# First layer of a sparse graph-attention kernel: whole-array transposes and Gram products with PSUM banks shared by two readers, in place of row tiles with one reader for each pair of banks

## Chip, cores and metric

The kernel runs on one core of a Trainium2 chip. The metric is the device time of one execution in microseconds; a run's time is that of its slowest core, here the only one. Before the change three runs took 906.34, 911.70 and 915.76 us, median 911.7.

## The reference

A two-layer graph attention block with residual and layer norms: 8 batches, 2048 nodes, 64 features, 4 heads of width 64. Cut to what matters:

```python
def _gat_layer(h, mask, b):
    scores = einsum('...nd,...md->...nm', h, h)
    attn = softmax(where(mask, scores, NEG))
    return einsum('...nm,...md->...nd', attn, h) + b
mask = adj + eye(N) > 0
h = einsum('bnc,hdc->bhnd', x, Wh)                 # first layer, 4 heads
z = leaky_relu(concat_heads(_gat_layer(h, mask, bh)), 0.2)
h2 = einsum('bnk,dk->bnd', z, Wo)                  # second layer, one head
z2 = leaky_relu(_gat_layer(h2, mask, bo), 0.2)
out = layernorm(x + layernorm(z2) * gamma + beta)
```

The adjacency matrix is random and uneven: the first nodes have many neighbours (hubs), the others few.

## The kernel before

The fast path is `fast_kernel`. The first 56 nodes are hubs and are handled densely. The other 1992 are cut into 166 sets of 12 nodes; each set has a list of at most 128 nodes that any of its members is linked to, found on VectorE (DVE) by repeated top-8 searches over packed bit keys (`pick`). A set's rows of x, all 8 batches at once, are fetched by an indirect DMA on the GpSimd queue (POOL, `gather`), 128 rows of 520 floats.

Four stages follow each other: the hub stage (dense scores of the hubs against all nodes, making of keys, first searches), the loop of the first layer, its drain, and the second layer. The change is in the first two.

The loop of the first layer (lines 1038 to 1106) handles one group g of two sets per iteration, 83 groups, with a software pipeline: iteration i has in hand the scores of group i+1, the values of group i, the transposes of group i+3 and so on. The order of the work on each engine is the order in which the program writes it. In one iteration TensorE (PE) does, in this order:

- `scores` (line 836): 16 matmuls in two row tiles of 64x128 (128 keys stationary, 48 columns moving), from `xTg`, the transposed rows, and `y`, the nodes' own features times the Gram matrices of the heads. They write the pair of PSUM banks `S`; `weigh` on DVE reads it, `lift` on ScalarE (ACT) exponentiates.
- `project` (line 538): eight 64x64 matmuls of 96 columns into the pair `C`; `leaky` (line 525) on ACT reads it, `leak` on DVE applies the slope.
- `columns` (line 819): eight 64x64 matmuls of 96 columns, the Gram matrices on the own rows, into the pair `T`; `keep_columns` on ACT copies them to `y`. The own rows come from `own_rows` on POOL, every second iteration, in three copies, two of them from one half of the partitions to the other (line 811).
- `second_maps` (line 895), `values` (line 861: 16 matmuls in column tiles of 128x64, 65 columns) and `second_rows` (line 911) into the pair `O`; `keep_own`, `invert` and `keep_rows` on DVE read it.
- `turn` (line 514): the gathered rows of two sets are transposed in 16 half transposes (64x128 stationary, 64 columns moving) into `T`; the next iteration copies them to `xTg` on ACT (line 1045).
- `turn_values` (line 880): eight transposes of 48 rows into the free columns of `C`; `keep_values` on ACT reads them.

An fp32 matmul appears as two passes in the trace, each with its own weight load; a transpose is one pass. PSUM has eight banks of 512 floats per partition, and the four pairs `S`, `C`, `T`, `O` take them all, each pair existing once. Before the change each pair is read by one engine: `S` and `O` by DVE, `C` and `T` by ACT. Before the change, also, the two gathers of a group are held back by explicit dependencies: the first until the scores of the iteration are done, the second until half of its values are (lines 1055 and 1075). Twelve row buffers exist.

DVE also works off the searches, a few steps per iteration (`some`), SP issues the loads of adjacency pieces (`load_adj`), of own rows for the residual (`load_own`) and the stores of the second layer's table, and POOL adds beta (`add_beta`, line 949).

Of the kernel before, what the change touches and what calls it, by code (L numbers as in the profile page):

```python
# [359 lines left out]
def fast_kernel(ctx: ExitStack, tc: tile.TileContext, x, adj, Wh, bh, Wo, bo, gamma, beta, out, flag):  # L360
# [29 lines left out]
    rowp = stage.enter_context(tc.tile_pool(name="rowp", bufs=12))  # L390
# [118 lines left out]
    def turn(tp, rows, j=0):  # L509

        for q in range(Q):
            c0 = (j * Q + q) * 64
            for r in range(2):
                nc.tensor.transpose(tp[:, r, c0:c0 + 64], rows[half(r), q, 1:1 + P], ident[half(r), half(r)])  # L514

    def turn_whole(tp, rows):

        for q in range(Q):
            nc.tensor.transpose(tp[:, q * P:(q + 1) * P], rows[:, q, 1:1 + P], ident)  # L519
# [12 lines left out]
    def project(ot, cat, n):  # L532

        for hp in range(HP):
            for s in range(2):
                for j in range(2):
                    h = 2 * hp + j
                    at = nc.tensor.matmul(cat[half(j), s, hp * n:(hp + 1) * n], whT[half(s), h * D:(h + 1) * D],  # L538
                                          ot[half(s), h, :], start=True, stop=True)
        return at  # L540
# [47 lines left out]
    def turn_x(i):  # L588
        tp = two(f"px{i}")
        turn(tp, xrow[i])  # L590
        nc.scalar.copy(xT[:, :, i * P:(i + 1) * P].rearrange("c q (r n) -> c r q n", r=2),
                       tp[:, :, :Q * 64].rearrange("c r (q n) -> c r q n", q=Q))
# [141 lines left out]
    def pick(r):  # L734
# [7 lines left out]
        def top(src, dst, last):  # L742
            todo.append(lambda: nc.vector.max(out=dst, in_=src))
            if not last:
                todo.append(lambda: nc.vector.match_replace(out=src, in_to_replace=dst, in_values=src, imm_value=-1.0))

        for j in range(ns):
            for i in range(KEEP // 8):
                k = j * KEEP + i * 8
                top(kv[:, j, :], cand[:, k:k + 8], i == KEEP // 8 - 1)  # L750
# [7 lines left out]
        for i in range(P // 8):  # L758
            top(cand, best[:, i * 8:(i + 1) * 8], i == P // 8 - 1)
# [35 lines left out]
    def gather(table, s, layer, new, behind=None):  # L795
        t = rows[layer, s] = new(f"g{layer}_{s}")
        g = nc.gpsimd.indirect_dma_start(out=t.rearrange("n q c -> n (q c)"), out_offset=None, in_=table,  # L797
                                         in_offset=bass.IndirectOffsetOnAxis(ap=index[:, s:s + 1], axis=0))
        if behind is not None:
            tc.add_manual_dep(g.ins, behind.ins.name, mybir.DependencyInfo(mybir.DependencyClass.Sync, mybir.DependencyReason.DATA),  # L800
                              reason="the gather's turn")

    def own_rows(m):

        t = held["x", m] = work.tile([P, 2 * GM], F32, tag="xo", name=f"xo{m}", bufs=2)
        v = t.rearrange("c (b s q k) -> c b s q k", b=2, s=2, q=Q)
        src = xT[:, :, HUB:].rearrange("c q (k s) -> c s q k", s=NS)
        nc.gpsimd.tensor_copy(v[:, 0], src[:, 4 * m:4 * m + 2])
        b0 = min(4 * m + 2, NS - 2)
        for r in range(2):  # L810
            nc.gpsimd.tensor_copy(v[half(r), 1], src[half(1 - r), b0:b0 + 2])  # L811

    def columns(g, tp):

        t = held["x", g // 2]
        for k in range(2):
            for r in range(2):
                for p in range(2):
                    nc.tensor.matmul(tp[half(p), r, k * GM:(k + 1) * GM], gram[half(r), g % 2 * 2 + k, half(r)],  # L819
                                     t[half(r), (p ^ r) * GM:((p ^ r) + 1) * GM], start=True, stop=True)  # L820

    def keep_columns(g, tp):
        if g % 2 == 0:
            held["y", g // 2] = work.tile([P, 2 * GM, H], F32, tag="yg", name=f"y{g // 2}", bufs=2)
        h0 = g % 2 * 2
        nc.scalar.copy(held["y", g // 2].rearrange("p (b n) h -> p b n h", b=2)[:, :, :, h0:h0 + 2],  # L826
                       tp[:, :, :2 * GM].rearrange("p b (k n) -> p b n k", k=2))

    def scores(g, sp):
        xt = held.pop(("T", 1, g))  # L830
        y = held["y", g // 2].rearrange("p n h -> p (n h)")
        for j in range(2):
            for q in range(Q):
                for p in range(2):
                    c0 = ((g % 2) ^ p) * GM * H + (j * Q + q) * M
                    at = nc.tensor.matmul(sp[:, p, (q * 2 + j) * M:(q * 2 + j + 1) * M], xt[half(p), j, q, :],  # L836
                                          y[half(p), c0:c0 + M], start=True, stop=True)
        return at
# [12 lines left out]
    OW = D + 2  # L851

    def values(g, op):
        e = es[g % 2]
        rw = [rows.pop((1, 2 * g + j)) for j in range(2)]
        for q in range(Q):
            for j in range(2):
                for p in range(2):
                    c0 = (p * 8 + q * 2 + j) * M
                    o0 = q * OW + p  # L860
                    at = nc.tensor.matmul(op[half(p), j, o0:o0 + K1], e[:, c0:c0 + 64], rw[j][:, q, sums(p)], start=True, stop=True)  # L861
                    if (q, j, p) == (1, 1, 1):
                        midway = at
        return midway

    def invert(g, op):
        v = op[:, :, :Q * OW].rearrange("a j (q c) -> a j q c", q=Q)
        osb = held["o", g] = work.tile([P, 2, Q, D], F32, tag="osb", name=f"osb{g}")
        r = rall[:, g, :].rearrange("a (j q) -> a j q", j=2)
        for p in range(2):  # L870
            nc.vector.reciprocal(r[half(p)], v[half(p), :, :, p * K1])
        nc.vector.tensor_tensor(osb, v[:, :, :, 1:K1], r.unsqueeze(3).to_broadcast([P, 2, Q, D]), OP.mult)  # L872

    def turn_values(g, pt):

        osb = held.pop(("o", g)).rearrange("a j q c -> a (j q c)")
        for w in range(4):
            for p in range(2):
                mine = slice(p * 64, p * 64 + M)
                at = nc.tensor.transpose(pt[:, p, w * M:(w + 1) * M], osb[mine, w * P:(w + 1) * P], ident[mine, mine])  # L880
        return at

    def keep_values(g, pt):

        ot = held["ot", g] = work.tile([P, H, GM], F32, tag="ot", name=f"otb{g}")
        nc.scalar.copy(ot.rearrange("c h (p m) -> c p h m", p=2), pt.rearrange("c p (m h) -> c p h m", h=H))  # L886
# [14 lines left out]

    def store_own(g):

        t = held["own", g]
# [3 lines left out]
    def second_rows(g, pr):  # L908
        t = held.pop(("own", g))
        for r in range(2):  # L910
            nc.tensor.transpose(pr[:, r, :], t[half(r)], ident[half(r), half(r)])  # L911

    def keep_rows(g, pr):
        r = rowts[g % 4]
        nc.vector.tensor_tensor(r[:GM, 1:1 + P].rearrange("n (p d) -> n p d", p=2), pr, bob[:GM], OP.add)
# [63 lines left out]
    for i in range(NB):  # L979
# [16 lines left out]
        for t in range(2):  # L996
# [12 lines left out]
            some(6)  # L1009
# [4 lines left out]
    for g in range(3):  # L1014
# [23 lines left out]
    for i in range(-4, NG + 4):  # L1038
        if i >= 1 and slow and len(slow) % 3:
            slow.pop(0)()  # L1040
        sp = one(f"s{i + 1}", "S")
        scored = scores(i + 1, sp) if 0 <= i + 1 < NG else None
        if 0 <= i + 2 < NG:
            t = held["T", 1, i + 2] = work.tile([P, 2, Q, P], F32, tag="xTg", name=f"xTg{i + 2}", bufs=2)
            nc.scalar.copy(t.rearrange("c j q (r n) -> c r (j q) n", r=2),  # L1045
                           held.pop(("tp", i + 2)).rearrange("c r (m n) -> c r m n", n=64))
        cat = one(f"cat{i}", "C")
        if 0 <= i - 2 < NG:
            project(held.pop(("ot", i - 2)), cat, GM)
            held["z", i - 2] = leaky(cat, GM, f"z{i - 2}")  # L1050
        if 0 <= i + 1 < NG:
            weigh(i + 1, sp)
        coming = i + LOOK if i > -3 else NG
        if coming < NG:
            gather(table1, 2 * coming, 1, rows_tile, scored)
        if turns():
            some(1)
        if i >= 0:
            if slow and len(slow) % 3 == 0:
# [4 lines left out]
        tp = one(f"t{i + 3}", "T")  # L1064
        if 0 <= i + 4 < NG + NG % 2:
            columns(i + 4, tp)
            keep_columns(i + 4, tp)
        if 0 <= i + 1 < NG:
            lift(i + 1)
        op = one(f"o{i}", "O")  # L1070
        if 0 <= i - 3 < NG:
            second_maps(i - 3, op[:, 0, 264:264 + GM])
        midway = values(i, op) if 0 <= i < NG else None
        if coming < NG:
            gather(table1, 2 * coming + 1, 1, rows_tile, midway)
        if 0 <= i - 4 < NG:
            second_rows(i - 4, op[:GM, :, 360:424])
        if 0 <= i - 2 < NG:
            leak(held["z", i - 2])
        if 0 <= i - 3 < NG:  # L1080
            keep_own(i - 3, op[:, 0, 264:264 + GM])
            store_own(i - 3)
        if i + 6 < NG and i % 2 == 0 and i >= -2:
            own_rows((i + 6) // 2)
        if i >= 10 and (i - 10) // 6 * 2 + (i - 10) % 6 // 2 <= NV and (i - 10) % 6 < 4:
            (add_beta if i % 2 else load_own)((i - 10) // 6 * 2 + (i - 10) % 6 // 2)
        if 0 <= i < NG:
            invert(i, op)
        if 0 <= i - 4 < NG:
            keep_rows(i - 4, op[:GM, :, 360:424])  # L1090
        for _ in range(6 if i < 0 else 3 if i < 16 else 2):
# [365 lines left out]
```

## Time and profile before

| | |
|---|---|
| time of the profiled execution | 906.34 us (the median of three runs is 911.7) |
| span of the profile | 904.5 us, 40409 instructions |
| busy: PE / weight loads / DVE / ACT / POOL | 769.5 / 698.0 / 615.1 / 513.4 / 487.5 us |
| mean granted TensorE clock | 0.924 |
| scores, line 836 | 2656 passes, 169.6 us busy |
| values, line 861 | 2656 passes, 96.5 us busy |
| half transposes, line 514 | 1328, 57.9 us busy |
| columns, line 819 | 1328 passes, 54.8 us busy |
| transposes of values, line 880 | 664, 33.8 us busy |
| whole transposes of the second layer, line 519 | 664, 82.0 us busy |
| gathers, line 797 | 332, 994 ns each on POOL |

The profile gives, for each engine, busy time; idle time is put down to what ended it. PE's matmuls are pipelined, so the busy time of a matmul overlaps that of its neighbours; distances between start times tell what one costs in a row of its like. The chain of waits follows the program back from its last instruction and lists, for each stretch of time, the work that everything after it waited for. The granted clock is TensorE's, as a share of full speed.

### The profile page before, as it was taken

What the parts mean: (1) busy time and instruction counts of PE and PEld (TensorE: products, weight loads), DVE (VectorE), ACT (ScalarE), POOL (GpSimd) and SP (SyncE); (2) the same over time, 40 slices, a digit from 0 to 9 for tenths busy, and PEclk for the clock granted to TensorE, in tenths of its full rate; (3) what the DMA queues carried; (4) which work ended last, traced back from release to release, by engine and by line L of the source; (5) the groups of instructions that cost most, each with busy time, mean ns of one, the idle gap of its engine ahead of it and who ended that gap; (6) DMA issues with size and microseconds to landing.
All of it is one profiled execution on the core that took longest, in us unless ns stands there. A gap on an engine that the chain in (4) does not pass through costs nothing.

```text
span 904.5 us, 40409 instructions
## 1 busy us (share of the span) xinstructions
PE 769.5 (85%) x17676; PEld 698.0 (77%) x17676; DVE 615.1 (68%) x1369; ACT 513.4 (57%) x878; POOL 487.5 (54%) x696
## 2 busy tenths in 40 slices
PE   2896776889889999999999999994799999998720
PEld 2675565778779999999999999993699989997720
DVE  3347867447677787767655556655338899999993
ACT  2332243345446666666666666662477887887721
POOL 5643140436555566655556665631777777777300
PEclk9998797669999999999999999997799999999965
DMA  8786350335444555555445455431888888888521
GB/s 176 227 239 201 107 149 4 98 101 146 112 129 130 143 142 148 149 156 143 136 127 153 140 152 153 138 83 43 255 273 248 268 263 270 270 252 249 170 49 30
DMA packets 81787, 145.11 MB, mean 160 GB/s; under 512 B 30146, under 2 KB 46466, under 8 KB 81602
## 3 DMA queue, kind: packets, MB, share of 16 engines
q0 software_dynamic: 26720, 88.55, 34.3%
q1 hardware_dynamic: 37842, 49.65, 18.0%
q10 hardware_dynamic: 17040, 4.25, 2.5%
q8 instruction: 140, 2.29, 1.0%
q14 instruction: 45, 0.37, 0.1%
HBM read 123.91 MB, written 18.48 MB: 157 GB/s over the span
## 4 chain that ended last, share of the span: by engine, by line
PE 61%; DVE 14%; DMA 11%; issue 4%; ACT 4%; POOL 2%; SPq 2%; DVEq 0%; POOLq 0%; ACTq 0%
PE s L836 15%; PE o L861 8%; DMA g<-table,index 5%; PE t L514 4%; PE t L819 4%; PE o L895 4%; PE cat L538 4%; DMA raw<-in_adj_dram 4%; PE t L519 4%; PE s L1156 3%; PE o L1188 3%; PE sh L1300 2%; PE cat L880 2%; PE e L1167 2%; PE o L911 2%
## 5 line engine op out<-in xcount | busy, mean ns | idle before, releaser
L797 POOL DMA_INDIRECT g<-table,index x332 | 330.1, 994 | 136.6 <-issue 54.3
L836 PE MATMUL s<-y,xTg 64*128 64x48 f32 x2656 | 169.6, 280 | 0.8 <-DVE rowt L660 0.8
L836 PEld LDWEIGHTS s<-y,xTg 64*128 64x128 f32 x2656 | 164.0, 197 | 1.7 <-DVE rowt L660 1.2
L842 DVE TENSOR_TENSOR e<-s,mask 128x768 f32<-128x768 f32 x83 | 79.3, 956 | 50.7 <-PE s L836 47.5
L525 ACT ACTIVATE z<-cat,bhp 128x192 f32<-128x192 f32 x166 | 60.9, 418 | 84.6 <-PE cat L538 79.3
L861 PE MATMUL o<-g,e 128*64 128x65 f32 x2656 | 96.5, 228 | 0.0
L519 PE MATMUL t<-ident,g 128*128 128x128 f32 x664 | 82.0, 277 | 12.8 <-DMA g<-table,index 12.8
L861 PEld LDWEIGHTS o<-g,e 128*64 128x64 f32 x2656 | 91.3, 144 | 0.6 <-issue 0.4
L811 POOL COPY xo<-xT 64x96 f32<-64x96 f32 x84 | 30.1, 359 | 113.5 <-DMA g<-table,index 101.5
L1343 ACT COPY xTg<-t 128x1024 f32<-128x1024 f32 x83 | 80.1, 1016 | 17.1 <-PE t L519 16.5
L1045 ACT COPY xTg<-t 128x1024 f32<-128x1024 f32 x83 | 84.4, 1017 | 2.9 <-PE t L514 2.9
L519 PEld LDWEIGHTS t<-ident,g 128*128 128x128 f32 x664 | 75.0, 143 | 14.2 <-issue 9.1
L849 ACT ACTIVATE e<-e,shifts 128x768 f32<-128x768 f32 x83 | 78.1, 941 | 0.7 <-DVE e L842 0.7
L886 ACT COPY otb<-cat 128x384 f32<-128x384 f32 x83 | 39.8, 479 | 66.5 <-PE cat L880 66.5
L604 ACT ACTIVATE e<-e,shifts 128x896 f32<-128x896 f32 x32 | 33.3, 1042 | 74.6 <-DVE e L601 65.2
L687 POOL TENSOR_SCALAR a<-raw 120x1024 bf16<-120x1024 int32 (+1 forms) x34 | 38.4, 1133 | 65.2 <-DMA raw<-in_adj_dram 36.4
L900 DVE COPY own<-o 128x96 f32<-128x96 f32 x83 | 21.3, 257 | 69.6 <-PE o L911 64.2
L530 DVE SCALAR_TENSOR_TENSOR z<-z 128x384 f32<-128x384 f32 x83 | 49.7, 599 | 27.3 <-ACT z L525 23.9
L819 PE MATMUL t<-xo,gram 64*64 64x96 f32 x1328 | 54.8, 260 | 14.2 <-DVE keys L715 5.3
L826 ACT COPY y<-t 128x384 f32<-128x384 f32 x83 | 43.5, 524 | 28.6 <-PE t L819 28.4
L514 PE MATMUL t<-ident,g 64*128 64x64 f32 x1328 | 57.9, 230 | 1.9 <-ACT y L826 1.9
L872 DVE TENSOR_TENSOR osb<-o,rall 128x512 f32<-128x512 f32 x83 | 57.4, 692 | 2.9
(171 smaller groups left out, 1488.3 us busy)
## 6 DMA issues: line engine op xcount, KB each, us to landing
raw<-in_adj_dram SPq DMA_DIRECT2D x32, 480.0 KB
table<-xb SPq DMA_DIRECT2D x22, 256.0 KB
xr_s<-table SPq DMA_DIRECT2D x21, 256.0 KB
g<-table,index POOLq DMA_INDIRECT x332
table<-x SPq DMA_DIRECT2D x16, 260.0 KB
x<-in_x_dram ACTq DMA_DIRECT2D x32, 128.0 KB
table<-rowt SPq DMA_DIRECT2D x166, 24.4 KB
xb<-in_x_dram SPq DMA_DIRECT2D x164, 24.0 KB
```

The lines of the kernel that those rows point to most:

```text
L514: nc.tensor.transpose(tp[:, r, c0:c0 + 64], rows[half(r), q, 1:1 + P], ident[half(r), half(r)])
L519: nc.tensor.transpose(tp[:, q * P:(q + 1) * P], rows[:, q, 1:1 + P], ident)
L525: nc.scalar.activation(z[:, hp], cat[:, :, hp * n:(hp + 1) * n], AF.Identity, bias=bhp[:, hp:hp + 1], scale=1.0)
L797: g = nc.gpsimd.indirect_dma_start(out=t.rearrange("n q c -> n (q c)"), out_offset=None, in_=table, in_offset=bass.IndirectOffsetOnAxis(ap ...
L819: nc.tensor.matmul(tp[half(p), r, k * GM:(k + 1) * GM], gram[half(r), g % 2 * 2 + k, half(r)], t[half(r), (p ^ r) * GM:((p ^ r) + 1) * GM] ...
L836: at = nc.tensor.matmul(sp[:, p, (q * 2 + j) * M:(q * 2 + j + 1) * M], xt[half(p), j, q, :], y[half(p), c0:c0 + M], start=True, stop=True)
L842: nc.vector.tensor_tensor(e[:, :16 * M].rearrange("p (a q n) -> p a q n", a=2, q=Q), sp[:, :, :8 * M].rearrange("p a (q n) -> p a q n", q= ...
L849: nc.scalar.activation(e[:, :16 * M], e[:, :16 * M], AF.Exp, bias=shifts[:, 0:1], scale=1.0)
L861: at = nc.tensor.matmul(op[half(p), j, o0:o0 + K1], e[:, c0:c0 + 64], rw[j][:, q, sums(p)], start=True, stop=True)
L872: nc.vector.tensor_tensor(osb, v[:, :, :, 1:K1], r.unsqueeze(3).to_broadcast([P, 2, Q, D]), OP.mult)
L1045: nc.scalar.copy(t.rearrange("c j q (r n) -> c r (j q) n", r=2), held.pop(("tp", i + 2)).rearrange("c r (m n) -> c r m n", n=64))
L1343: nc.scalar.copy(t, tp)
```

## The change

Five things change together.

- `turn` makes whole 128x128 transposes, four per set, for x in the hub stage and for the gathered rows in the loop. The two sets of a group are turned at the end of the iteration, with `turn_values` between them.
- `columns` becomes two matmuls with the whole 128x128 block-diagonal Gram matrix and 192 moving columns; `own_rows` becomes one copy. `second_rows` becomes one transpose, `turn_values` four transposes of 112 rows.
- The pairs are shared differently. `columns`, `second_maps` and `second_rows` write `C`, next to `project`; ACT (`leaky`, `keep_columns`) and DVE (`keep_own`, `keep_rows`) read it. `turn_values` writes `O`, next to `values`; DVE (`invert`) and ACT (`keep_values`, now two instructions) read it. `T` holds the turned rows alone.
- Project, second maps and second rows each come one iteration earlier, and the loop ends one iteration earlier. The order on each engine is rewritten accordingly.
- The gathers lose their explicit dependencies and stand together behind the values; ten row buffers take the place of twelve. The searches' steps are queued in pairs (maximum and replacement), half as many per turn. Own rows for the residual are loaded from iteration 30 on, one load or one addition per iteration.

```diff
-    rowp = stage.enter_context(tc.tile_pool(name="rowp", bufs=12))
+    rowp = stage.enter_context(tc.tile_pool(name="rowp", bufs=10))
...
-    def turn(tp, rows, j=0):
...
-            for r in range(2):
-                nc.tensor.transpose(tp[:, r, c0:c0 + 64], rows[half(r), q, 1:1 + P], ident[half(r), half(r)])
+    def turn(tp, rows):
...
             nc.tensor.transpose(tp[:, q * P:(q + 1) * P], rows[:, q, 1:1 + P], ident)
...
-    def columns(g, tp):
...
-                    nc.tensor.matmul(tp[half(p), r, k * GM:(k + 1) * GM], gram[half(r), g % 2 * 2 + k, half(r)],
-                                     t[half(r), (p ^ r) * GM:((p ^ r) + 1) * GM], start=True, stop=True)
+    def columns(g, cat):
+        n = min(4, NS - 4 * (g // 2)) * 48
         for k in range(2):
+            nc.tensor.matmul(cat[:, k, 2 * GM:2 * GM + n], gram[:, g % 2 * 2 + k, :], held["x", g // 2][:, :n], start=True, stop=True)
...
         for w in range(4):
-            for p in range(2):
-                mine = slice(p * 64, p * 64 + M)
-                at = nc.tensor.transpose(pt[:, p, w * M:(w + 1) * M], osb[mine, w * P:(w + 1) * P], ident[mine, mine])
+            nc.tensor.transpose(turned(op)[:, w, :], osb[:112, w].rearrange("a s c -> a (s c)"), ident[:112, :112])
```

The order of the loop's body after the change (conditions on i left out):

```python
scores(i + 1, sp); weigh(i + 1, sp)
project(ot[i - 1], cat, GM); z[i - 1] = leaky(cat, GM)
nc.scalar.copy(xTg[i + 2], tp[i + 2])
lift(i + 1)
values(i, op); invert(i, op)
gather(2 * (i + LOOK)); gather(2 * (i + LOOK) + 1)
own_rows((i + 6) // 2)
load_own((i - 30) // 2) or add_beta((i - 30) // 2)
leak(z[i - 1])
more(1)
second_maps(i - 2, cat); second_rows(i - 3, cat); columns(i + 4, cat)
keep_own(i - 2, cat); keep_rows(i - 3, cat)
some(1) twice
keep_columns(i + 4, cat)
turn(tp[:, 0, :], rows[2 * (i + 3)])
turn_values(i, op); keep_values(i, op)
turn(tp[:, 1, :], rows[2 * (i + 3) + 1])
```

## The prediction

> **What bounds the kernel now.** The page's slices came first: PE stands at 9 from the thirteenth slice of 22.6 us to the twenty-seventh with the granted clock at 9, so the middle of the run belongs to TensorE. A table by stage then cuts the span where the start times of the score matmuls (line 836) put the borders: hub stage to 145 us, first layer 145 to 610, drain to 641, second layer to the end.
>
> ```profile
> PE   2896776889889999999999999994799999998720
> ...
> PEclk9998797669999999999999999997799999999965
> ```
> ```profile
> core 0: us, PE busy (x) PEld busy (x) DVE busy (x) ACT busy (x) POOL busy (x), PEclk, DMA share, GB/s
> ...
> 152.50:271.10 118.60, 103.99 (x2027) 93.70 (x2025) 71.68 (x186) 53.97 (x93) 58.87 (x87) 0.80 0.39 111
> 271.10:609.70 338.60, 335.74 (x8555) 315.79 (x8551) 226.04 (x560) 223.66 (x395) 198.54 (x306) 0.99 0.50 140
> 609.70:641.00 31.30, 14.21 (x254) 10.95 (x250) 14.97 (x39) 7.39 (x16) 10.68 (x15) 0.72 0.35 102
> ```
>
> From 271 to 610 us PE is busy 99%, DVE and ACT two thirds. Whether that is work or overlap of pipelined records the chain of waits tells; one iteration of it:
>
> ```profile
> 325.85 1.79 PE s L836 x32
> 327.63 0.49 PE cat L538 x16
> 328.12 0.33 PE t L819 x16
> 328.45 0.48 PE o L895 x8
> 328.94 0.93 PE o L861 x32
> 329.87 0.19 PE o L911 x2
> 330.06 0.49 PE t L514 x16
> 330.55 0.24 PE cat L880 x8
> 330.79 1.79 PE s L836 x32
> ```
>
> Nothing but PE: 4.94 us per iteration, the sum of its pieces. The 83 iterations start at 152.5 and the last at 609.7. The first 16 take 118.6 us (79.0 at 4.94), at a mean clock of 0.80; the other 66 take 338.6 (326.0 at 4.94, so 12.6 lost). PE hardly waits in the latter, and what it waits for is line 811:
>
> ```profile
> PE t L819 <- POOL xo L811: 1.9, 6, 0.5
> PE t L819 <- DVE keysi L770: 0.6, 1, 0.6
> ```
>
> So whatever changes PE's sum changes the period one for one, until another engine takes over at some higher period.
>
> **The change on PE.** Start times of single matmuls in iterations at full clock give the price of each form. Row or column tiles that run together count as one group: line 836 one pair per 0.111 us; 538 and 819 one quad of 96 columns per 0.083; 895 one pair per 0.083; 861 one pair per 0.058; 514 one pair of 64 columns per 0.061; 880 one pair of 48 per 0.059. Wherever the tile shape changes, the first two groups come late: 836 to 538 by 0.09 and 0.05, 819 to 895 by 0.11 and 0.05, 861 to 911 by 0.10 and 0.03. These prices rebuild 1.78 + 0.33 + 0.33 + 0.33 + 0.93 + 0.06 + 0.49 + 0.24 + 0.43 = 4.92 of the 4.94.
>
> Scores, project, values and second maps keep their shapes. The rest:
>
> - Transposes of gathered rows: 16 half transposes (8 pairs, 0.49) become 8 whole ones. Line 519 is the same instruction in the second layer, 1.75 us for 16:
>
> ```profile
> 661.02 1.75 PE t L519 x16
> ```
>  That is 0.109 each, 0.87 in all: +0.38.
> - Columns: 4 quad passes of 96 columns (0.33) become 4 passes (2 matmuls of two passes) of the whole array with 192 columns. No row has that form. Line 598 moves 224 columns per pass at 0.189, line 519 moves 128 at 0.109; by that slope 192 cost 0.163, so 0.65; two of the quads' 96-column passes would make 0.166, the wider pass 0.189, and these are the bounds (a gain is excluded: more columns stream than before). I take 0.163: +0.32. The Trainium skill, "TensorEngine Tiling (Array Packing)", Theoretical Speedup, gives up to 2 times for each dimension of at most 64; an estimate at its limit, 4 times, makes whole-array columns 1.32, this step +0.99 and the result some 55 us later. Here the form before and the form after make the same number of passes, and only the columns of a pass double.
> - turn_values: 4 pairs of 48 columns (0.24) become 4 transposes of 112 columns, 0.096 each by the same slope: 0.38, +0.14.
> - second_rows: one pair (0.06) becomes one 128-column transpose (0.11): +0.05.
> - Shape changes: three per iteration (0.43) become four: into 64x64 (0.14), into 128x64 (0.16), into the whole array (line 1322 to 1167: 0.10 and 0.06, so 0.16), back to 64x128 for scores (line 615 to 598: 0.10 and 0.10, so 0.20). 0.66: +0.23.
>
> Sum +1.12, period 6.06.
>
> **Who could be late next.** I laid one new iteration out by hand, zero at the last score pair. PE: project to 0.5, values to 1.64, second maps from 1.70, columns 2.3 to 2.9 (landing 3.05), first turn 2.9 to 3.3, turn_values 3.4 to 3.7, second turn to 4.1, scores to 6.06. Against this:
> - The cat bank pair now has two readers. In this kernel a reader waits for writes to other columns of the same bank; keep_own, which reads what line 895 wrote, waits for line 911:
>
> ```profile
> DVE own L900 <- PE o L911: 64.2, 70, 5.2
> ```
>  So second maps wait for leaky (ACT, 0.31 after project's last start, 0.73 long: done at 1.56, seen at 1.62 against 1.70; 0.08 of cover, values hide it). The Trainium skill, "PSUM — Partial Sum Buffer", "PSUM bank collisions raise a hardware error", wants even two reads of one bank by different engines kept apart; no row here shows that, and by it keep_columns on ACT would always wait for keep_rows on DVE.
> - Even so: DVE runs weigh 0.37 to 1.33, invert (two of 0.20, one of 0.69) 1.93 to 3.04, leak to 3.6, keep_own and keep_rows to 4.15, two selection steps (0.92 each) to 6.0, weigh again at 6.43. Turn_values on PE waits for invert, 0.25 of cover.
> - ACT: leaky, copy of the turned rows to 2.5 (1.02; the first turn at 2.9 waits for it, 0.35 of cover), lift to 3.36, keep_columns from there or, at worst, only when keep_rows has left the same bank, 4.2 to 4.72, then keep_values as two instructions in place of one (0.73 like line 525) to 5.45. The next project needs it at 6.26: 0.8 of cover even so.
> - POOL: both gathers wait for values of their own iteration (10 row buffers, five sets of two), are issued 1.9 to 3.9, land some 4.7 later as in the chain ("DMA g<-table,index" pieces of 4.2 to 4.9), and are wanted two iterations on, after 15: nothing. The two partition-shifted copies of line 811, which the trace shows waiting for gathers to land, go; one copy of 192 columns (two of line 808, 0.7) replaces three.
>
> ```profile
> POOL xo L811 <- DMA g<-table,index: 101.5, 35, 3.8
> ```
>  That gives back most of the 12.6 us of loss; I take 9.
> - SP: loads of own rows move later (iterations 30 to 74) with the same count; line 949 idles 0.1 us in all, so nothing. The top-8 steps in pairs are the same instructions.
>
> **Sum.** Steady: 66 x 1.12 = +74, less 9: +65. First 16 iterations: 16 x 1.12 / 0.80 = +22, less about 8, because line 811's stall (the 9.9 us iteration at 220) and half of two waits for the key steps (2 x 1.22 us on DVE, now beside second maps and columns) are covered: +14. Hub stage: 16 times 0.19 + 0.15 for whole transposes of x, if exposed +5; but at 100 to 140 us its chain is DVE, ACT and score matmuls, so +1. Drain: one iteration less, about 3 us as between 618 and 622: -3. Second layer: same instructions. Together +77. The profiled run took 906.34 (904.5 span, 1.8 around it) and is the fastest of three, so 983; the median stands 5.4 above it, so 989 for a median.
>
> Bounds: at the low side +0.96 an iteration (shape changes +0.07), all 12.6 given back, first part +5, drain -5: +51, 963. At the high side columns at 0.189 and leaky uncovered by 0.1, +1.33 an iteration, 5 given back, +25 and +5 in front, no gain in the drain: +113, 1025.
>
> **Rivals.**
> 1. ACT or DVE closes the loop through the shared banks (project, leaky, columns, keep_rows, keep_columns, keep_values, next project). It decides once this runs 0.8 us later than laid out; each 0.5 beyond adds 83 x 0.5 = 42 us: 1031. For it: six hand-offs between engines with covers of 0.08 to 0.8. Against: all three engines' busy sums stay under 5.1 of 6.06. 14%.
> 2. The other side: PE is bound by its number of instructions, not by columns. Then 130 an iteration at 4.94 / 130 = 0.038 us become 105, the period 4.0, and 82 x 0.94 = 77 us go: 835. It decides if a whole transpose costs less than 0.061, as a pair does. Against it are the 0.109 of line 519 and the 0.111 of line 836, which differ from the 0.058 of 861 at equal count. 2%.
> 3. The extra work falls into time lost anyway, mostly in the slow first part: the loop lost 40 + 12.6 us. If 40 of it is filled, 77 - 40 = +37: 949. For it: the clock is at half in 145 to 169 us, so PE may not be what decides there. Against: iterations of 9.5 to 10.1 there are just twice 4.94, PE's own sum. 6%.
>
> **Numbers.** Forecast 78%, its own range 963 to 1025; rivals 14, 2 and 6%. The range takes in the near side of rivals 1 and 3: 956 to 1031. A measurement cannot tell less than 1% from no change: faster 2% (rival 2), same 1%, slower 97%.
>
> **What would show it.** Scores of neighbouring iterations 6.0 to 6.1 us apart in the steady part, line 519's form at 0.109 in the first layer, columns near 0.163 a pass, PE busy near 99%, no idle of PE before columns. Wrong if PE shows idle in the steady part ended by ACT or DVE (rival 1), or if whole-array passes come closer than 0.1 us (rival 2).

## The result, and the profile after

The changed kernel is slower. Beside four runs of the kernel before on the same chip (median 913.73 us, 906.34 to 920.58) its four runs have the median 958.16 us (955.39 to 962.27): a ratio of 1.0518, interval 1.0428 to 1.0608. The ratio is one of means of fast runs, so the run of 920.58 us, more than 1.5% above the fastest, is left out of it. The profiled execution took 955.54 us, its span 953.6 us at a mean granted clock of 0.957. Against the span of before, 904.5 us at 0.924, that is +49.1 us; the forecast was +77.

Line numbers have moved: scores are line 818 now, project 531, values 843, second maps 877, second rows 887, columns 804, whole transposes 512, transposes of values 860.

The slices of the page first, busy tenths of PE and the granted clock:

```profile
PE   2976788899999999999999999999399999998840
...
PEclk9989998999999999999999999999699999999975
```

PE's row of nines is twenty slices long, fifteen before; it begins earlier and ends later. The second row holds what the forecast had not expected: slices seven to nine, where the first layer begins, stand at 8, 9, 9 where before they stood at 7, 6, 6.

The table by stage, cut as before (first 16 iterations, the other 66, then drain and second layer together), puts numbers on both. Columns: the stretch and its length, busy time and count of PE, weight loads, DVE, ACT, POOL, then the granted clock, DMA share and GB/s.

```profile
152.30:265.00 112.70, 103.37 (x1664) 91.75 (x1664) 75.07 (x189) 55.52 (x112) 51.15 (x70) 0.97 0.39 107
265.00:661.10 396.10, 394.08 (x6923) 361.88 (x6922) 229.01 (x587) 223.63 (x461) 185.96 (x244) 1.00 0.43 121
661.10:953.60 292.50, 225.71 (x5438) 204.04 (x5437) 222.15 (x414) 186.04 (x334) 169.26 (x171) 0.90 0.68 204
```

| stretch | before | after | difference | forecast |
|---|---|---|---|---|
| up to the first scores | 152.5 | 152.3 | -0.2 | +1 |
| first 16 iterations | 118.6 | 112.7 | -5.9 | +14 |
| other 66 iterations | 338.6 | 396.1 | +57.5 | +65 |
| drain and second layer | 294.8 | 292.5 | -2.3 | -3 |
| span | 904.5 | 953.6 | +49.1 | +77 |

The 66 iterations carry the loss; the largest error of the forecast is in the 16 before them. In those PE is busy 103.4 us at a clock of 0.97, where before it was busy 104.0 at 0.80: more work, in the same busy time.

One iteration in the chain of waits (start, length, what), in which again nothing but PE stands:

```profile
500.67 1.92 PE s L818 x32
502.59 0.49 PE cat L531 x16
503.08 1.08 PE o L843 x32
504.16 0.33 PE cat L877 x8
504.49 0.24 PE cat L887
504.74 0.65 PE cat L804 x4
505.39 0.44 PE t L512 x4
505.83 0.39 PE o L860 x4
506.21 0.44 PE t L512 x4
506.65 1.92 PE s L818 x32
```

The period is 5.98 us, 1.04 more than 4.94. What PE waits for between 265 and 661 us (waiting line, what it waited for; total us, times, longest) is one short list:

```profile
PE pb L761 <- ACT xTg L1027: 1.3, 2, 0.7
PE o L860 <- DVE osb L851: 0.7, 1, 0.7
```

### The profile page after: what moved, and what is told of

Its sections match the earlier page's. It is cut to its first block, busy times and chain, and to the rows that moved or that the text cites. A ratio compares the mean times of both kernels' runs of the same rounds, so it can differ in the third digit from the quotient of the medians.

```text
span 953.6 us, 36242 instructions
## 1 busy us (share of the span) xinstructions
PE 831.1 (87%) x15525; PEld 741.5 (78%) x15525; DVE 611.8 (64%) x1369; ACT 514.2 (54%) x961; POOL 467.5 (49%) x612
## 4 chain that ended last, share of the span: by engine, by line
PE 70%; DVE 11%; DMA 7%; ACT 5%; issue 3%; POOL 2%; SPq 1%; DVEq 0%; POOLq 0%; ACTq 0%
PE s L818 17%; PE t L512 12%; PE o L843 9%; PE cat L804 6%; PE cat L531 4%; DMA raw<-in_adj_dram 4%; PE o L860 3%; PE s L1130 3%; PE o L1162 3%; PE cat L877 3%; PE e L1141 2%; PE cat L887 2%; PE sh L1274 2%; ACT xTg L1317 2%; DVE e L592 1%
## 5 line engine op out<-in xcount | busy, mean ns | idle before, releaser
L512 PE MATMUL t<-ident,g 128*128 128x128 f32 x1328 | 183.2, 276 | 15.8 <-DMA gh<-table 10.5
L512 PEld LDWEIGHTS t<-ident,g 128*128 128x128 f32 x1328 | 155.7, 143 | 20.4 <-issue 13.7
L818 PEld LDWEIGHTS s<-y,xTg 64*128 64x128 f32 x2656 | 154.7, 188 | 13.8 <-issue 13.6
L810 ACT COPY y<-cat 128x384 f32<-128x384 f32 (+1 forms) x80 | 40.2, 502 | 62.4 <-PE o L860 40.2
L850 DVE RECIPROCAL rall<-o 64x8 f32<-64x8 f32 x166 | 34.0, 205 | 56.0 <-PE o L843 54.7
L804 PE MATMUL cat<-xo,gram 128*128 128x192 f32 (+1 forms) x320 | 66.3, 331 | 0.0
L804 PEld LDWEIGHTS cat<-xo,gram 128*128 128x128 f32 x320 | 54.3, 204 | 0.2
L1162 PE MATMUL o<-g,es 128*32 128x65 f32 x2656 | 48.1, 224 | 5.0 <-DVE y_s L1185 4.5
L592 DVE TENSOR_TENSOR e<-sh,maskh 128x896 f32<-128x896 f32 x32 | 34.8, 1087 | 24.3 <-PE sh L589 20.0
L1162 PEld LDWEIGHTS o<-g,es 128*32 128x32 f32 x2656 | 45.1, 112 | 5.9 <-issue 3.8
```

The lines of the kernel that those rows point to most:

```text
L804: nc.tensor.matmul(cat[:, k, 2 * GM:2 * GM + n], gram[:, g % 2 * 2 + k, :], held["x", g // 2][:, :n], start=True, stop=True)
L1162: nc.tensor.matmul(op[t * 32:(t + 1) * 32, f, k * W2 + p:k * W2 + p + K1], e[:, 2 * q + p, k, :], rw[:, q, sums(p)], start=(a == 0 and k = ...
```

## The experiments

Three questions were open. Is the price list of PE's forms right, piece by piece? Why did the first 16 iterations become shorter although each does more? And what is the stall at line 811 worth? For the second the main theory is that the clock came up because of the whole transposes; its rivals are that it came up because of the work before the first scores, or because of another part of the change. An expectation that gives theories letters says itself what each forecasts.

The kernels ran on three chips, and each is compared with the kernel before on its own chip: medians 917.2 us on the first, 1101.8 on the second, 1102.6 on the third. That difference between chips is itself a result, told below. Lengths and half-clock times of stretches are read from one profile of each run. The half-clock time given for a stretch is the sum of the clock records of 0.5 in it.

**1. Whole transposes alone.** The kernel before, with the loop's 16 half transposes as eight whole ones (a condition that always holds in the loop is left out of the lines).

```diff
-            nc.scalar.copy(t.rearrange("c j q (r n) -> c r (j q) n", r=2),
-                           held.pop(("tp", i + 2)).rearrange("c r (m n) -> c r m n", n=64))
+            nc.scalar.copy(t.rearrange("c j q n -> c j (q n)"), held.pop(("tp", i + 2)))
...
-                turn(tp, rows[1, 2 * (i + 3) + j], j)
+                turn_whole(tp[:, j, :], rows[1, 2 * (i + 3) + j])
```

> The kernel before, with the eight whole 128x128 transposes per iteration in the first layer and nothing else of the change. Price theory: +0.38 us for the transposes and about +0.3 for two more changes of tile shape, so a steady period near 5.6 us in place of 4.94 and 66 x 0.69 = +45 us in the steady part, less a few us of stall. For the first 16 iterations (118.6 us before, 54 of the stretch from 145 to 271 us at half clock): theory A, that the granted clock comes up when TensorE streams columns for most of the time, which whole transposes do and score passes (48 columns for a 128-column load) do not, wants them clearly shorter than 118.6, near 105 with little half clock. Theory B, that the clock and the first part follow the stalls (copies waiting for gathers, gathers held back, searches on DVE), all of which stay here, wants 118.6 + 16 x 0.69 / 0.8 = 132.

Measured: 948.56 us, ratio 1.0345 (1.0279 to 1.0411); period 5.61. Its chain of waits shows where the 0.67 goes: the transposes' piece, 0.49 before, and the pieces around it as they were.

```profile
400.28 0.38 PE cat L880 x8
...
404.68 0.19 PE o L911 x2
404.87 1.02 PE t L519 x8
```

The piece is 0.53 longer; the rest is the change of shape towards the next form, `turn_values` (0.38 in place of 0.24, the first of these lines). By the prediction's prices, +0.38 and two changes of shape at 0.16, it is 0.69 to 0.70. The first 16 iterations and the other 66 (columns as in the table by stage):

```profile
159.10:277.00 117.90, 106.09 (x1896) 92.51 (x1895) 72.99 (x184) 53.93 (x93) 59.16 (x87) 0.89 0.41 113
277.00:647.30 370.30, 369.66 (x8037) 338.19 (x8033) 223.15 (x559) 221.83 (x395) 197.65 (x306) 1.00 0.46 127
```

The first 16 take 117.9 us, between theory A's 105 and theory B's 132, and their half-clock time is 25.6 us (46.9 in the profile before): the clock comes up 19 us after the first scores and then falls only twice more, for 3.4 us each.

The other 66 take 370.3 us, that is 66 x 5.61 and nothing more: the 12.6 us lost beside the period before are gone, though this kernel still makes the three copies of `own_rows` and line 811 still waits (in the steady part; waiting line, releaser; us, times, longest; the kernel before, then this run):

```profile
POOL xo L811 <- DMA g<-table,index: 95.2, 32, 3.8
...
POOL xo L811 <- DMA g<-table,index: 80.1, 31, 3.9
```

So on this chip a longer period is enough to hide that wait. Run 9, on another chip, loses time beside the same period.

**2. Whole transposes in the first iterations only.** The edit of run 1, for groups 0 to 7; the others are turned in halves.

```diff
+                if (i + 3) < 8:
+                    turn_whole(tp[:, j, :], rows[1, 2 * (i + 3) + j])
+                else:
+                    turn(tp, rows[1, 2 * (i + 3) + j], j)
```

> The kernel before, with whole transposes for groups 0 to 7 alone, half transposes for the other 75. Theory A: the clock comes up early in the loop, the first 16 iterations take some 100 to 110 us in place of 118.6, the steady period stays 4.94: 895 to 905 us against 907 to 912. Theory B: 8 x 0.69 / 0.6 = 9 us are added, 918.

Measured: 918.36 us, ratio 1.0005 (0.9954 to 1.0056). The time is theory B's 918. Half-clock time in the first 16 iterations is 45.4 us, their length 120.5. A few iterations of whole transposes bring no lasting gain: once the halves resume, phases of half clock begin at 220, 247, 261 and 274 us. A kernel that uses the whole form as a starter does not keep the clock.

**3. Whole-array columns alone.** The kernel before with the change's `columns`, `keep_columns` and the single copy in `own_rows`.

```diff
-        for r in range(2):
-            nc.gpsimd.tensor_copy(v[half(r), 1], src[half(1 - r), b0:b0 + 2])
...
-                    nc.tensor.matmul(tp[half(p), r, k * GM:(k + 1) * GM], gram[half(r), g % 2 * 2 + k, half(r)],
-                                     t[half(r), (p ^ r) * GM:((p ^ r) + 1) * GM], start=True, stop=True)
+            nc.tensor.matmul(tp[:, k, :n], gram[:, g % 2 * 2 + k, :], held["x", g // 2][:, :n], start=True, stop=True)
```

> The kernel before, with whole-array columns (192 moving columns, two matmuls) and the one copy of own rows that goes with them, nothing else of the change. Price theory: +0.32 for the columns and +0.16 for one more change of shape, a steady period of 5.42 us; no copy waits for a gather any more, so the 12.6 us lost in the steady part shrink to 3 or less: 66 x 0.48 - 9 = +23 us there. First 16 iterations: theory A, shorter than 118.6 because whole-array columns stream all the time; theory B, shorter by the copies' stalls alone, about 5 us, and longer by 16 x 0.48 / 0.8 = 10.

Measured: 938.26 us, ratio 1.0202 (1.0132 to 1.0272); period 5.46, +0.52, all of it in the columns' piece of the chain (0.33 before):

```profile
400.55 0.85 PE t L814 x4
```

The first 16 iterations take 124.5 us, near theory B's sum (118.6 less 5 plus 10), with 49.0 us at half clock; the other 66 take 66 x 5.46 less 0.9. So the columns cost 0.52 where 0.48 was priced, this edit too gives the steady loss back, and it does not raise the clock.

**4. The clock under one form at a time.** A probe that computes nothing of the reference: seven stretches, each of one form of instruction (the quads alone have gaps in between, of 0.6 to 1.1 us), about 10 us of DVE work between them. In order: score passes, half transposes, whole transposes, whole columns, values, quads, score passes again.

```diff
+    for n, (form, count) in enumerate([(scores, 130), (half_turns, 260), (whole_turns, 180), (whole_columns, 70),
+                                       (values, 200), (quads, 150), (scores, 130)]):
+        for k in range(count):
+            form(ps, k)
```

> Not the reference's computation: seven stretches of TensorE work of one form each, with some 10 us of TensorE idle between them, and the granted clock read off each. Order: score passes (64x128 pairs, 48 columns), half transposes (64x128 pairs, 64 columns), whole transposes, whole-array columns (192), values (128x64 pairs, 65 columns), 64x64 quads of 96 columns, score passes again. Theory A: the score passes stay at half clock for their whole stretch (about 29 us at half clock, 14 at full), all others come up within some 7 us. Theory B: every form, being without a gap, comes up within some 7 us, score passes too.

The windows of the seven stretches; here the columns are the length, PE, weight loads, DVE, POOL, then clock, DMA share, GB/s, in the order given above:

```profile
5.50:61.20 55.70, 55.68 (x520) 55.52 (x520) 0.00 (x0) 0.00 (x0) 1.00 0.01 1
71.60:89.60 18.00, 17.97 (x520) 17.83 (x520) 0.00 (x0) 0.00 (x0) 1.00 0.01 4
100.00:122.50 22.50, 22.50 (x180) 22.28 (x180) 0.00 (x0) 0.00 (x0) 0.88 0.00 1
132.90:157.60 24.70, 24.62 (x140) 24.35 (x140) 0.01 (x1) 0.00 (x0) 0.93 0.00 1
168.00:194.20 26.20, 26.19 (x800) 26.05 (x800) 0.00 (x0) 0.00 (x0) 0.89 0.02 4
204.60:238.30 33.70, 28.46 (x1200) 26.84 (x1200) 0.00 (x0) 0.00 (x0) 0.95 0.02 4
248.70:304.40 55.70, 55.69 (x520) 55.52 (x520) 0.00 (x0) 0.00 (x0) 0.50 0.00 1
```

Both stretches of score passes take 55.7 us for 260 pairs of passes, 0.214 us each, against 0.111 in the loop: half clock from beginning to end, although PE has no gap. (The clock has no record before 75 us, so a row can show 1.00 for time ahead of that, as it does for the first stretch of score passes against its own durations.) All other forms came up, 3 to 6 us after their start, the half transposes among them. That is theory A's forecast; its 29 us at half clock left out the second pass of each matmul. But the half transposes by themselves do not keep the clock down; what a loop gets seems to depend on its mixture. The score passes are over a third of the loop's time (1.79 of 4.94 us), and they are the form that does not bring the clock up.

**5. Work before the first scores.** The kernel before, with 46 transposes of the identity, unused otherwise, in PE's idle places in iterations -3 to -1.

```diff
+    def fill(bank, n):
+        for k in range(n):
+            nc.tensor.transpose(bank[:, k % 2, k % 4 * P:(k % 4 + 1) * P], ident, ident)
...
+        if i in (-2, -1):
+            fill(sp, 8)
...
+        if -4 < i < 0:
+            spare = one(f"w{i}", "O")
+            fill(spare, 6)
```

> The kernel before, with 46 transposes of the identity added to the prologue of the first layer (iterations -3 to -1, into banks that are free there), so that TensorE has no gap of half a microsecond and more before the first scores; their results are not used. Theory A2: score passes at half clock do not release it, so what counts is whether the clock is already up when the first scores start; it is then up, the half clock in the first 16 iterations falls from 46.9 us to under 20, and the run gets 8 to 18 us shorter (ratio 0.98 to 0.99). Theory B: the clock falls whenever the loop stalls, as before, and the run is level or up to 5 us longer for the added transposes.

Measured (second chip): 1097.11 us, ratio 0.999 (0.9951 to 1.0028). The clock does come up, at 155.4 us, before the first scores at 159.5, and the first two iterations take 5.17 and 6.00 us in place of 5.96 and 9.72 (run 7, the same chip). But it falls again at 179.3 us; half-clock time in the first 16 is 41.0 us, where run 7 has 52.6 and theory A2 wanted under 20. As with run 2, a warm start is not kept.

**6. Whole transposes and whole columns together.** Runs 1 and 3 in one kernel (the edits above, no more).

> The kernel before, with whole transposes and whole-array columns together, and all else as before. Price theory: the steady period is the sum of the two steps measured alone, 4.94 + 0.67 + 0.52 = 6.13 us, and less than 2 us is lost beside it. If forms alone bring the clock up, the first 16 iterations have under 15 us at half clock as in the changed kernel (6.8); if it needs the changed kernel's gapless prologue or its other order, they keep 25 to 49 us as in the two single steps.

Measured (second chip): 1128.54 us, ratio 1.0235 (1.019 to 1.0279); period 6.13 us. That is 4.94 + 0.67 + 0.52 to the hundredth: the prices add. Half-clock time in the first 16 is 28.2 us, as with the whole transposes alone, and far from the changed kernel's 6.8. The two forms are thus not the whole of the cause.

**7 and 8. Both kernels again, unchanged, on the second chip.**

> The kernel before, profiled a second time: how far the first 16 iterations (118.6 us), their half clock (46.9 us) and the hub stage (first scores at 152.5 us) differ from one execution to the next. Theory A and B both want 47 us of half clock give or take 10.

> The changed kernel, profiled a second time: first 16 iterations 112.7 us, half clock 6.8 us, steady period 5.98 us, first scores at 152.3 us. Both theories want the same again, half clock under 20 us.

Measured: 1104.42 and 1095.37 us, one execution of each. The first-16 stretch repeats what the first profiles showed: 125.2 us with 52.6 at half clock before, 111.9 with 6.8 after. So does the changed kernel's steady part, 396.2 us at 5.98. The steady part of the kernel before does not: 391.6 us here, 338.6 in the first profile. Two rows of run 7, the steady stretch and the stretch from the last iteration on, show it; the third row is the latter stretch in the first profile (columns as in the first table by stage):

```profile
285.60:677.20 391.60, 371.55 (x8555) 342.71 (x8553) 223.44 (x562) 223.93 (x395) 200.73 (x308) 0.94 0.45 121
...
677.20:1102.60 425.40, 276.17 (x5488) 233.74 (x5484) 225.06 (x420) 185.97 (x334) 166.10 (x172) 0.84 0.51 140
...
609.70:904.50 294.80, 226.01 (x5490) 204.91 (x5486) 224.64 (x420) 186.77 (x334) 169.39 (x172) 0.90 0.67 202
```

The same 8555 passes are busy for 371.6 us, not 335.7, as 47.8 us are at half clock, and PE is idle for 20 us. Drain and second layer take 425 us in place of 295 at 140 GB/s in place of 202, with the same instructions. Here the changed kernel is level with the kernel before: its steady part is as long as on the first chip, where that of the kernel before is 53 us longer.

**9. A warm start and whole transposes.** Runs 5 and 1 together.

> The kernel before with both: the added transposes of the identity ahead of the first scores, and whole transposes of the gathered rows throughout. Theory C, two causes: gaps of TensorE in the prologue let the loop start at half clock (cured by the added transposes, as b_warm showed at 155 to 179 us), and after each later stall the clock comes back slowly where the transposes are in row tiles (cured by whole ones, as b_turn_whole showed after 178 us). Then half clock in the first 16 iterations is under 12 us, as in the changed kernel, and they take 16 x 5.61 + 16 to 20 = 106 to 110 us. If it is something else in the changed kernel (its order, its gathers), 25 us of half clock stay and 118 us or more. Steady period 5.61 either way.

Measured (third chip): 1099.11 us, ratio 0.9974 (0.9933 to 1.0015); half-clock time in the first 16 is 20.5 us, between the values expected, and their length, 118.8 us, is that of the second theory. The warm start adds little to the whole transposes (25.6 in run 1), and the changed kernel's 6.8 is still not reached. The steady part misses the 5.61 that was expected:

```profile
279.00:663.50 384.50, 380.18 (x8035) 344.15 (x8033) 222.64 (x558) 224.79 (x395) 198.99 (x306) 1.00 0.45 122
```

That is 14 us more than 66 x 5.61. Line 811 waits here too, 71.8 us in all; which part of the 14 us is its doing no run separates.

**10. The changed kernel with half transposes.** Both sets are turned in halves, behind `turn_values`; all else as changed.

```diff
-            turn(tp[:, 0, :], rows[1, 2 * (i + 3)])
...
-            turn(tp[:, 1, :], rows[1, 2 * (i + 3) + 1])
+            for j in range(2):
+                for q in range(Q):
+                    for r in range(2):
+                        nc.tensor.transpose(tp[:, r, (j * Q + q) * 64:(j * Q + q + 1) * 64],
+                                            rows[1, 2 * (i + 3) + j][half(r), q, 1:1 + P], ident[half(r), half(r)])
```

> The changed kernel with the gathered rows turned in half transposes again (both sets behind turn_values), all else as changed. Price theory: -0.38 us for the transposes and level in changes of shape (into the row tile before the turns in place of before the scores), 5.60 us, and up to 0.2 more where turn_values now waits for invert. Theory C: no half clock at the start (the prologue has no gaps), but 10 to 25 us of it after the stalls of the next ten iterations, against 6.8. A theory that whole transposes do not matter to the clock: 7 us as in the changed kernel. Steady part 66 x 0.38 = 25 us shorter than the changed kernel's.

Measured (third chip): 1086.34 us, ratio 0.9831 (0.9784 to 0.9878). Its first two iterations with the 5 us ahead of them, its first 16 and the other 66:

```profile
152.50:173.00 20.50, 20.27 (x180) 18.18 (x182) 4.75 (x11) 8.09 (x13) 5.70 (x7) 0.50 0.17 44
...
157.80:273.10 115.30, 107.15 (x1796) 93.01 (x1794) 74.17 (x187) 54.94 (x109) 51.20 (x70) 0.89 0.40 107
273.10:660.10 387.00, 383.00 (x7447) 335.42 (x7443) 230.46 (x590) 225.26 (x462) 186.28 (x245) 1.00 0.46 124
```

The first two rows bear on the question of the clock for this kernel. With the half form back, half-clock time rises from 6.8 to 25.4 us (157.8 to 173.0 in one piece), the mean clock falls from 0.97 to 0.89, and the stretch is longer than the 111.9 and 112.7 us of the changed kernel, although each of its iterations in the steady part is shorter. Theory C had the amount nearly right and the place wrong: 15 of the 25 us lie at the start, where it wanted none. There PE is busy 20.27 of 20.50 us at half clock, so work without gaps ahead of the first scores is not enough. The edit also moves the first set's transposes behind `turn_values`; that order costs PE no idle time in these 20.5 us, but form and order were not tried apart.

The period is 5.84 us, outside what was expected, and that miss is instructive. In the single instructions, `turn_values` starts 0.35 us after the last column pass, where a column pass takes 0.16 in a row of its like. The DVE instruction it needs, line 851, ends 0.056 us before it starts. The half transposes now stand behind it, so the work that covered `invert` is gone, and some 0.19 us of each iteration is a wait. In the changed kernel the first set's whole transposes lie between, and the same DVE instruction ends 0.30 us ahead of `turn_values` (505.36 against 505.66 us): the forecast's 0.25 of cover, measured.

**11. The stall of line 811, alone.** The kernel before, with the two copies from one half of the partitions to the other on ACT.

```diff
-            nc.gpsimd.tensor_copy(v[half(r), 1], src[half(1 - r), b0:b0 + 2])
+            nc.scalar.copy(v[half(r), 1], src[half(1 - r), b0:b0 + 2])
```

> The kernel before with the two partition-shifted copies of own rows on ScalarE in place of GpSimd, nothing else. If these copies' waits for gathers are what the steady part lost (12 us beside 66 x 4.94), the loss falls under 4 us, the iteration near 220 us loses its 5 us, and the run is 8 to 16 us shorter (ratio 0.983 to 0.991). If the wait is the data's and goes with the copies to ScalarE, ScalarE stalls instead, everything behind it on that engine with it, and the run is longer by more than 10 us.

Measured (third chip): 1070.97 us, ratio 0.9691 (0.9651 to 0.9731), faster than both kernels, and by more than expected. The steady stretch:

```profile
286.10:644.20 358.10, 345.80 (x8555) 320.89 (x8553) 222.65 (x561) 249.51 (x457) 173.60 (x244) 1.00 0.49 132
```

Compared with the kernel before on the second chip (run 7, a like one), the stretch is 33.5 us shorter for the same 8555 passes: 25.8 us of it are PE's busy time, at a clock of 1.00 in place of 0.94, and 7.7 us its idle time. So more of it comes from the clock than from the waiting, as far as profiles of two chips tell. What POOL waits for in this stretch (columns as for the waits above) no longer has line 811 in it; nearly all of it is gathers that wait for their turn:

```profile
POOL g L797 <- PE s L836: 86.5, 63, 2.1
POOL g L797 <- PE o L861: 77.8, 62, 3.0
```

The edit also takes 27 us of work off POOL, and a rival remains that this and not the wait made the gain. Beside 66 x 4.94 the stretch still loses 32 us, so the edit gave back about half of what such a chip loses there. On a chip like that of the first profile it was not tried; there the steady part loses 12.6 us in all, so it could give no more than that in this stretch.

**12. Run 11 with the warm start of run 5.**

> The kernel before with both the copies on ScalarE and the added transposes ahead of the first scores. Theory C: 3 to 8 us shorter than with the copies alone, since the first two iterations run at full clock (5.2 and 6.0 us in place of 6.0 and 10.1) and fewer stalls follow that could bring it down again. Theory B: level with the copies alone.

Measured (third chip): 1070.61 us, ratio 0.9691 (0.9652 to 0.973), level with run 11. Half-clock time in the first 16 iterations falls from 57.2 to 34.1 us and that stretch from 126.2 to 119.2, but the whole shows nothing of it that can be measured. A third time, warming PE ahead of the loop is not worth its instructions.

## Why the prediction was right or wrong

The direction, the place and the mechanism were right: PE's own sum closes the loop, and the period grows with it. The time, 958, lies below the forecast's own range and is inside the whole range by 2 us, on the side that was added for rival 3; that is luck, as rival 3's means was not what happened. The forecast was some 31 us too high. Where those come from, step by step (in spans, 27.9 of them):

- **Transposes, columns, transposes of values, second rows.** Confirmed. In the steady part of the changed kernel a whole transpose follows the one before by 0.109 us, a column pass by 0.162 to 0.165 (0.163 was taken by the slope; the two bounds given beside it, 0.166 and 0.189, both lie above it and above what was measured), a transpose of 112 columns by 0.096. Runs 1 and 3 measured two of the steps alone, run 6 their sum.
- **The Trainium skill's limit of packing.** "TensorEngine Tiling (Array Packing)", Theoretical Speedup, would have made whole-array columns +0.99 by the estimate at its limit. Run 3 shows +0.52 with its shape changes; the wide pass doubles the columns that stream and not more.
- **Shape changes.** Too dear by 0.08 an iteration. The term of 0.20 for the way back to scores was read where values in column tiles come first and passes of 224 columns follow (line 615 to 598); here, from whole transposes to passes of 48 columns, it is 0.09 and 0.04. The other three are 0.15, 0.16 and 0.14. So the sum is 0.58, not 0.66. All other pieces together took what was priced, so the period is 5.98, not 6.06, and 66 x 0.08 = 5.3 us are explained.
- **The stalls of the steady part.** 9 of 12.6 us were to come back; 11.2 did (12.6 to 1.4). The reason given was that the copies of line 811 go. Run 1 shows that on that chip they need not: a period of 5.61 hides them. Where one copy takes their place, in runs 3 and 6 and in the changed kernel on the second chip, 1.5 us at most are lost.
- **Who could be late next.** Nobody. PE is idle 2.0 us in 396.1, and the two waits listed above are all. The covers of 0.08 to 0.8 us held, the smallest too; run 10 shows what it costs to take one away. The worst case laid out for ACT is what happens: `keep_columns` (line 810) starts 0.09 us after `keep_rows` on DVE (line 891) has ended, in every iteration of the steady part, though both only read the bank.

```profile
506.27 0.51 ACT L810 COPY y<-cat 128x384 f32<-128x384 f32 x1 [0.66 <-DVE rowt L891]
```
  PE does not wait for it, as was forecast. Rival 1 fell with that. Rival 2 fell with the 0.109 us of a whole transpose.
- **First 16 iterations: the step that failed.** It was "16 x 1.12 / 0.80 = +22", less about 8 for covered stalls. The stalls gave 5.3 back (PE idle 14.6 us before, 9.3 after), 2.7 less than taken. But the +22 became -0.6, PE's busy time going from 104.0 to 103.4 us. The mean clock of before, 0.80, was carried over as if the change could not touch it. It rose to 0.97: half-clock time fell from 46.9 to 6.8 us. At PE's busy share of 0.88 and 0.92 half clock cost 46.9 x 0.88 / 2 = 20.6 us before and 3.1 after; 16 x 1.04 = 16.6 of new work less 17.5 is -0.9, against the -0.6 measured. Run 10 points to the whole transposes for much of this in the changed kernel (with their place in the order, which moved too), and run 1 shows that they do a part of it in the kernel before; run 3 shows that the columns alone do not.
- **Rival 3** had the right stretch and the wrong means. It let the extra work fill idle time; what absorbed it was the clock. The reading held against it, that iterations of 9.5 to 10.1 us are PE's own sum at half clock, holds for one of five: that of 10.13 us is at half clock throughout, the others for 0 to 5.9 us, and they have 1.9 to 2.7 us of idle time and up to 12 passes more.
- **Hub stage and drain:** -0.2 and -2.3, against +1 and -3.

What stays open: in the kernel before, whole transposes alone, with columns or with a warm start leave 20.5 to 28.2 us of half clock, the changed kernel 6.8 in both of its profiles. Something else in it, the order of the forms, the forms or the order before the first scores, or the gathers without dependencies, must do the rest; no run separates these. Nor does any show why line 811 waits for gathers it doesn't read; that its instruction does, and that the copies cause no such wait on ACT, is what the traces show.

## What to carry to other kernels

Where PE closes a loop, price each form by the distance between starts in a row of its like and add 0.13 to 0.16 us, here, for each change of tile shape; the growth of the period came out at 1.04 for 1.12 forecast, and for two parts tried alone at 0.67 for 0.69 and 0.52 for 0.48. Don't divide new work by an old mean clock: ask which forms the change puts in place of which, since the clock under the new mixture may be another one. And look for small copies that wait for a transfer they don't need: here moving two of them to another engine gained 3% on a chip where the kernel before takes 1102 us, and no other edit gained as much there.

## What the runs showed of the hardware

- A stretch of nothing but score passes (fp32, 64 x 128 weights, 48 columns moving) stays at half clock for 55.7 us without a gap, twice; other forms come up within 3 to 6 us.
- Times on different chips differ. The same program took 913.7 to 917.2 us on two measurements and 1101.8 and 1102.6 on two other chips: on one of the latter +130 us are in drain and second layer (140 GB/s in place of 202), +53 in the steady part. Whether that is the chip or what else ran on it at the time is not shown. The verdict on the change depends on it: 5% slower on the one, level on the other (1095.4, one execution, beside a median of 1101.8).
- Idle time of PE can come with half clock, and need not: in the steady part 20 us of idle came with 47.8 us at half clock (run 7), 15 with 41.0 (run 5), but 12 with 3.4 (run 11). What decides it is not shown.
- PE busy without a gap can stay at half clock in a mixture too: 20.27 of 20.50 us before and in the first two iterations of run 10.
